# Two 1x1 convolutions of a residual block, both with seven products for eight, run in turn on halves of a tile

## The chip, the cores and the metric

The kernel runs on one core of a Trainium2 chip. The metric is the device time of one launch in microseconds (us); lower is better. Most runs of a kernel agree within 0.2%. Each result below is the median of four or five runs (three in the first table), one of them profiled.

## The reference, cut to what matters

Two residual blocks of the same shape follow each other, on an fp32 tensor of 64 images, 1024 channels, 14 x 14 pixels:

```python
def block(x, w1, b1, g1, be1, w2, b2, g2, be2, w3, b3, g3, be3, residual_scale):
    out = relu(bn(conv1x1(x, w1, b1), g1, be1))        # 1024 -> 256 channels
    out = relu(bn(conv3x3(out, w2, b2), g2, be2))      # 256 -> 256
    out = bn(conv1x1(out, w3, b3), g3, be3)            # 256 -> 1024
    return relu(x + softplus(residual_scale) * out)
# bn uses the mean and variance of the whole batch, so each convolution must end
# before its normalisation can start
```

## The kernel before: the parts the argument touches

A tile is two images (392 pixels, `PX`) of all channels, 32 tiles in all. The stages, in order: first convolution of block 0 ("first stage"); its 3x3 convolution; a Gram stage that gets the statistics of the third convolution without running it; then the **fused stage**, which runs the third convolution of block 0 and, on the tile just finished, the first convolution of block 1; then 3x3, Gram and third convolution of block 1.

The first convolution multiplies 2 x 2 blocks (channel halves by pixel blocks) with seven products for eight, in the manner of Strassen and Winograd. Its seven products share banks of PSUM: a running bank (`bu`, two of them in turn) into which P1, P6, P7 and P4 add one after the other, and a second shared bank (`bp`) for P5 and P3. Between two products on a bank ScalarE copies the partial sum out or VectorE evicts it. The pixel blocks are two whole tiles, so a matmul is 392 columns wide.

```python
# kernel before, fused stage (cut): third convolution plain, in tiles; first in pairs of tiles
def residual(psum, pool, b, t, w3, aff, made=()):
    ...
    for o in range(CS):                                   # 8 output groups
        ps = made[o] if o < len(made) else conv3(psum, t, o, w3)
        v = xt[:, o, :]
        nc.vector.scalar_tensor_tensor(v, ps, scale[:, o : o + 1], v, ALU.mult, ALU.add)
        nc.scalar.activation(v, v, AF.Relu, bias=shift[:, o : o + 1])
        ...
made = [conv3(psum, 0, o, w3) for o in range(2)]          # early, during the statistics
...
# kernel before, first stage (cut): order of the products, ScalarE not pinned
for t in range(2, T, 2):
    now.t23(); now.t1()                                   # sums of inputs on VectorE
    now.p2(); now.p6()
    ...
    after.p1()                                            # next pair
    now.p7(); now.p5(); now.c22(); now.p4(); now.p3()
```

`tc.keep_in_program_order` pins an instruction among the others so marked on its engine; without it a scheduler orders VectorE and ScalarE by its own forecast. Within one engine, instructions run in the order that results.

## Time and profile before

| of the kernel before | |
|---|---|
| time, median | 2220.75 us (2220.22 to 2221.67, 3 runs) |
| span of the profiled run | 2217.4 us |
| first stage, up to the first normalisation on ScalarE | 312.4 us |
| scaling of the Gram matrix to the next normalisation: statistics and fused stage | 760.0 to 1411.0, 651.0 us |

The prediction below shows the busy times, the windows and the instruction costs (its "fourth window" is the last of the three rows that it shows). Lines of the timeline: the columns are start, duration, engine, line, operation, output<-input, shapes, number of records, and in brackets the idle time before and what ended it. A record is one entry of the trace; each matmul in fp32 leaves two.

```profile
297.27 0.93 PE L126 MATMUL bu<-t,w1s 128*128 128x392 f32 x2 [0.64 <-ACT u L189]
...
767.83 3.63 PE L126 MATMUL bu<-zmean,w 128*128 128x2 f32 x32
771.32 2.16 PE L126 MATMUL bu<-ones,q 128*128 128x1 f32 x16
```

The first is from 30 to 309 us, where the first stage runs its seven products. The other two are the small matmuls of the statistics: 32 records in 3.63 us, 16 in 2.16.

### The profile page before, as it was taken

The numbers are of one execution on the slowest core, as the hardware profiler recorded it, in microseconds if no ns is written. First come the engines' busy times: TensorE is split into PE (matmuls) and PEld (weight loads), VectorE is DVE, ScalarE is ACT, GpSimd is POOL, SyncE is SP. The second block draws the span as 40 slices with busy tenths as digits, with TensorE's granted clock in tenths as the row PEclk, the third lists the DMA queues.
The fourth block names the chain that finished last, engine by engine and source line by source line (L and its number), as shares of the span: only waits on it lengthen the run. The fifth ranks groups of instructions, "written<-read, shape, count | busy, mean of one in ns | idle before, by whom it ended". The sixth has DMA issues, their size and how long they took to land.

```text
span 2217.4 us, 22513 instructions
## 1 busy us (share of the span) xinstructions
PE 2144.0 (97%) x8984; PEld 1578.6 (71%) x8984; DVE 1343.1 (61%) x2091; ACT 585.8 (26%) x943; POOL 60.9 (3%) x126
## 2 busy tenths in 40 slices
PE   8999979999989999999999999799999799999997
PEld 5555559999988855555555555599999797555554
DVE  4766567787775455554555555678878534444443
ACT  1111142111105032332223323511111221444443
POOL 0100000000001000000000000000000000000000
PEclk9999989999999999999999999899999899999999
DMA  7755425555543443443434432355555401778884
GB/s 276 267 204 206 176 84 190 187 193 190 187 158 121 159 167 149 171 175 145 175 152 171 171 146 116 148 186 194 190 186 194 195 12 59 291 290 302 306 319 176
DMA packets 43977, 409.13 MB, mean 185 GB/s; under 512 B 5216, under 2 KB 5472, under 8 KB 11104
## 3 DMA queue, kind: packets, MB, share of 16 engines
q1 hardware_dynamic: 29376, 286.80, 35.9%
q0 software_dynamic: 13056, 118.50, 13.1%
q10 hardware_dynamic: 1440, 2.40, 0.3%
q8 instruction: 71, 1.16, 0.2%
q14 instruction: 34, 0.28, 0.0%
HBM read 289.18 MB, written 118.49 MB: 184 GB/s over the span
## 4 chain that ended last, share of the span: by engine, by line
PE 83%; issue 12%; DVE 2%; ACT 1%; POOL 1%; DMA 1%; POOLq 0%; ACTq 0%; DVEq 0%; SPq 0%
PE ps L126 19%; PE bu L126 15%; PE bp L126 7%; PE ps L343 6%; PE ps L349 6%; PE ps L338 6%; PE ps L345 6%; PE ps L351 6%; PE bx L126 4%; PE bx L439 4%; PE bp L440 2%; PE ps L451 2%; ACT y L264 1%; POOL out L519 1%; DVE spare L155 0%
## 5 line engine op out<-in xcount | busy, mean ns | idle before, releaser
L126 PE MATMUL ps<-y,w 128*128 128x392 f32 x2048 | 685.6, 494 | 0.2 <-DVE x L515 0.2
L126 PEld LDWEIGHTS ps<-y,w 128*128 128x128 f32 x2048 | 390.4, 191 | 285.9 <-issue 2.8
L515 DVE SCALAR_TENSOR_TENSOR x<-ps,scale,x 128x392 f32<-128x392 f32 x512 | 316.0, 624 | 274.8 <-PE ps L126 273.5
L516 ACT ACTIVATE x<-x,shift 128x392 f32<-128x392 f32 x512 | 314.7, 622 | 435.5 <-DVE x L515 435.5
L371 DVE TENSOR_TENSOR f<-ps,ms 128x448 f32<-128x448 f32 x192 | 113.2, 600 | 148.3 <-PE ps L351 81.8
L338 PE MATMUL ps<-sums,u 128*128 128x224 f32 (+1 forms) x768 | 172.1, 347 | 25.4 <-DVE sums L318 12.7
L126 PE MATMUL bu<-t,w1s 128*128 128x392 f32 x496 | 173.6, 493 | 1.3 <-ACT u L189 1.3
L343 PE MATMUL ps<-r,u 128*128 128x224 f32 (+1 forms) x768 | 173.6, 347 | 0.0
L349 PE MATMUL ps<-r,u 128*128 128x224 f32 (+1 forms) x768 | 172.8, 346 | 0.0
L338 PEld LDWEIGHTS ps<-sums,u 128*128 128x128 f32 x768 | 137.3, 190 | 26.8 <-issue 13.3
L345 PE MATMUL ps<-r,u 128*128 128x192 f32 (+1 forms) x768 | 154.1, 322 | 0.0
L351 PE MATMUL ps<-r,u 128*128 128x192 f32 (+1 forms) x768 | 153.3, 321 | 0.0
L362 ACT ACTIVATE ms<-ps 128x448 f32<-128x448 f32 (+1 forms) x80 | 41.9, 524 | 391.7 <-PE ps L338 391.7
L126 PEld LDWEIGHTS bu<-t,w1s 128*128 128x128 f32 x496 | 94.1, 190 | 71.0 <-ACT u L189 2.8
L343 PEld LDWEIGHTS ps<-r,u 128*128 128x128 f32 x768 | 141.8, 190 | 1.3
L349 PEld LDWEIGHTS ps<-r,u 128*128 128x128 f32 x768 | 136.7, 189 | 1.4
L345 PEld LDWEIGHTS ps<-r,u 128*128 128x128 f32 x768 | 132.9, 189 | 1.2
L351 PEld LDWEIGHTS ps<-r,u 128*128 128x128 f32 x768 | 131.8, 188 | 1.0
L189 ACT ACTIVATE u<-bu 128x392 f32<-128x392 f32 x93 | 46.2, 497 | 303.2 <-PE bu L126 303.2
L439 PE MATMUL bx<-zt 128*128 128x257 f32 x392 | 119.3, 386 | 4.1 <-DVE zt L453 4.0
L453 DVE TENSOR_TENSOR zt<-ps,crow 128x512 f32<-128x512 f32 x98 | 66.2, 690 | 93.3 <-PE ps L451 93.2
L264 ACT ACTIVATE y<-y,shift,scale 128x1568 f32<-128x1568 f32 x64 | 103.6, 1682 | 6.4 <-DVE shift L556 6.4
(134 smaller groups left out, 2115.3 us busy)
## 6 DMA issues: line engine op xcount, KB each, us to landing
u<-u SPq DMA_DIRECT2D x96, 1280.0 KB, 5.5
x<-in_x SPq DMA_DIRECT2D x62, 1568.0 KB, 6.7
mid<-x POOLq DMA_DIRECT2D x32, 1568.0 KB, 5.5
x<-mid SPq DMA_DIRECT2D x32, 1568.0 KB, 8.5
out<-x POOLq DMA_DIRECT2D x32, 1568.0 KB, 7.7
u<-y POOLq DMA_DIRECT2D x24, 320.0 KB, 5.9
u<-spare POOLq DMA_DIRECT2D x24, 320.0 KB, 3.0
x<-in_x SPq DMA_DIRECT2D x4, 784.0 KB, 7.2
```

The costliest lines, as they stand in the source:

```text
L126: tc.keep_in_program_order(nc.tensor.matmul(*args, **kw))
L264: nc.scalar.activation(y, y, AF.Relu, bias=shift[:, s : s + 1], scale=scale[:, s : s + 1])
L338: nc.tensor.matmul(m[:, o, :n], w(s, D1D2), sums[:, s].rearrange("p l c -> p (l c)"), start=(s == 0), stop=(s == MS - 1),)
L343: nc.tensor.matmul(odd, w(s, D1), r[:, s, :, WH:], start=(s == 0), stop=False)
L345: nc.tensor.matmul(odd[:, :, : WH - 1], w(s, D3), r[:, s, :, WH + 1 :], start=False, stop=(s == MS - 1))
L349: nc.tensor.matmul(even, w(s, D2), r[:, s, :, :WH], start=(s == 0), stop=False)
L351: nc.tensor.matmul(even[:, :, 1:], w(s, D0), r[:, s, :, : WH - 1], start=False, stop=(s == MS - 1))
L371: nc.vector.tensor_tensor(f[:, o].rearrange("p r (i q c) -> p q (r i) c", i=GI, q=2)[:, :, :lines], eos[o][:, :, :n].rearrange("p q (l c) ...
L439: nc.tensor.matmul(g0, zt[:, c, 0:P], zt[:, c, :], start=first, stop=last)
L453: nc.vector.tensor_tensor(zt[:, :, :M], tp.rearrange("p (c m) -> p c m", c=CH), crow[:, None, :].to_broadcast([P, CH, M]), ALU.subtract,)
L515: nc.vector.scalar_tensor_tensor(v, ps, scale[:, o : o + 1], v, ALU.mult, ALU.add)
L516: nc.scalar.activation(v, v, AF.Relu, bias=shift[:, o : o + 1])
```

## The change

The intent: give the third convolution of the fused stage seven products for eight too. For that a tile is cut into two halves of 196 pixels, which serve as the pixel blocks; one matmul of the first convolution alternates with one of the third, the first lagging 42 products (28 of a tile and `LAG`) behind. A unit is one set of seven products of the third convolution, two of a tile's eight output groups; a tile has four. ScalarE's order is pinned, so that the relus of a unit stand behind the next unit's second copy; GpSimd takes two of the additions. One generator, `stream`, gives the order of products for both convolutions, so the first stage gets this order too, with whole tiles. Core of the diff, with cuts:

```diff
+LAG = 14
-    class Conv1:
+    class Seven:
+        def p1(self):
+            self.y = self.bank("y", 2)
+            yield from self.product(self.y, self.a[0][0], self.b[0][0], True)
+            self.after1()
 ...
+    def stream(items):
+        before = None
+        for now in items:
+            yield from now.p1()
+            if before is not None:
+                yield from before.p3()
+                yield from before.p4()
+            yield from now.p6()
+            if before is not None:
+                before.end()
+            yield from now.p2()
+            yield from now.p5()
+            yield from now.p7()
+            before = now
 ...
+    def act(*args, **kw):
+        tc.keep_in_program_order(nc.scalar.activation(*args, **kw))
 ...
+    class Conv1(Seven):
+        def after1(self):
+            self.u1 = self.saved("au1")
+            self.t1, self.t2, self.t3 = (self.sum(i) for i in range(1, 4))
+            nc.vector.tensor_sub(self.t3, self.b[1][1], self.b[0][1])
+            nc.vector.tensor_add(self.t2, self.t3, self.b[0][0])
+            nc.vector.tensor_sub(self.t1, self.b[0][1], self.b[0][0])
+        def after6(self):
+            self.u2 = self.saved("au2")
+            self.t4 = self.sum(4)
+            nc.vector.tensor_sub(self.t4, self.b[1][0], self.t2)
+        def after7(self):
+            self.result(1, 1, self.p, self.saved("au3"))
 ...
+    class Conv3(Seven):
+        def after7(self):
+            u3 = self.saved(...)
+            nc.gpsimd.tensor_add(self.part(1, 1), self.part(1, 1), u3)
+        def after3(self):
+            self.add(0, 1, self.p)
+            v = self.xt[:, self.o[0], :]
+            nc.gpsimd.tensor_add(v, v, self.u12)
+        def end(self):
+            for row in range(2):
+                self.relu(row)
 ...
+        a, c = stream(first_convs()), stream(last_convs())
+        step = 7 * CS // 2
+        for i in range(step + LAG):
+            next(c)
+        while True:
+            more = next(a, "end"), next(c, "end")
 ...
-                made = [conv3(psum, 0, o, w3) for o in range(2)]
+                    made = [conv3(psum, 0, o, w3) for o in range(2)] if b == 1 else ()
```

## The prediction

> **What bounds the kernel now.** I read the page's busy times first, then a table of windows cut at the stage borders, then the chain of waits, then single instructions on the timeline.
>
> ```profile
> PE 2144.0 (97%) x8984; PEld 1578.6 (71%) x8984; DVE 1343.1 (61%) x2091; ACT 585.8 (26%) x943; POOL 60.9 (3%) x126
> PE 83%; issue 12%; DVE 2%; ACT 1%; POOL 1%; DMA 1%; POOLq 0%; ACTq 0%; DVEq 0%; SPq 0%
> ```
>
> TensorE is busy for 97% of the span and carries the chain. The changed ("fused") stage, third convolution of layer 0 with first convolution of layer 1, is the fourth window; the first row is the first stage, which the change reorders. Columns: length, busy time with count per engine, granted clock, DMA share, GB/s.
>
> ```profile
> 0.00:310.00 310.00, 300.37 (x904) 172.70 (x904) 191.67 (x250) 45.78 (x87) 13.69 (x30) 1.00 0.56 204
> 760.00:781.00 21.00, 20.84 (x88) 13.46 (x88) 11.89 (x39) 1.77 (x5) 0.00 (x0) 0.92 0.22 77
> 781.00:1407.00 626.00, 624.33 (x1896) 359.58 (x1894) 331.96 (x429) 187.82 (x318) 17.01 (x32) 1.00 0.40 154
> ```
>
> In the fused window TensorE idles 1.7 of 626 us at full clock: the stage is its count of matmul records times their spacing. VectorE has half its time free, ScalarE 70%, and 154 GB/s leaves DMA out of it. Each fp32 matmul leaves two records. Spacing against width, from the chain (8 records) and from starts on the timeline (4 records a row):
>
> ```profile
> 43.84 2.63 PE bp L126 x8
> ...
> 650.45 0.73 PE L338 MATMUL ps<-sums,u 128*128 128x168 f32 x4
> 651.02 0.74 PE L343 MATMUL ps<-r,u 128*128 128x168 f32 x4
> ...
> 334.10 0.92 PE L338 MATMUL ps<-sums,u 128*128 128x224 f32 x4
> 334.85 0.93 PE L343 MATMUL ps<-r,u 128*128 128x224 f32 x4
> ```
>
> 392 columns: 2.634/8 = 329.2 ns a record. 168: 0.57/4 = 142.5. 224: 0.757/4 = 189.3. The new width, 196, lies midway: 166 ns, so 332 ns a matmul. Transposes of 128 columns follow each other at 0.44/4 = 110 ns, so weight loading does not limit 166. The engines that must follow have these costs (busy, mean ns):
>
> ```profile
> L515 DVE SCALAR_TENSOR_TENSOR x<-ps,scale,x 128x392 f32<-128x392 f32 x512 | 316.0, 624 | 274.8 <-PE ps L126 273.5
> L318 DVE TENSOR_TENSOR sums<-r 128x448 f32<-128x448 f32 x80 | 49.0, 617 | 0.6
> L219 DVE TENSOR_TENSOR t<-x 128x1568 f32<-128x1568 f32 x31 | 55.5, 1792 | 51.0 <-PE bu L126 38.6 <-ACT x L516 11.0 <-DMA x<-in_x 1.4
> L201 DVE BATCH_NORM_STATS2 stats<-y 128x6 f32<-128x392 f32 x124 | 70.3, 567 | 46.3 <-ACT y L196 43.7
> L189 ACT ACTIVATE u<-bu 128x392 f32<-128x392 f32 x93 | 46.2, 497 | 303.2 <-PE bu L126 303.2
> L196 ACT ACTIVATE y<-bu,par 128x392 f32<-128x392 f32 x31 | 18.2, 587 | 92.5 <-PE bu L126 92.5
> L516 ACT ACTIVATE x<-x,shift 128x392 f32<-128x392 f32 x512 | 314.7, 622 | 435.5 <-DVE x L515 435.5
> ```
>
> **What the Trainium skill says.** "ScalarE: Activation LUTs", section "What ACT_TABLE_LOAD costs": 186 ns + 0.833 ns per element, 93 ns more per per-partition operand, back-to-back instructions overlap by 93 ns. The trace agrees (497 without, 587 with). "VectorE: DVE Perf Modes", section "The TRN2 errata": an fp32 tensor_tensor takes (N+151)/0.96 ns; the trace has 617 against 624 at 448 and 1792 against 1791 at 1568. "GPSIMD Engine Reference", section 3.1: the same add takes 4497 ns at 2048 elements, 2.6 cycles an element. No GpSimd add is in this trace; scaled, my estimate is 0.5 us at 196 and 0.9 us at 392. "SBUF — State Buffer", section "Who interferes with whom": a VectorE instruction with two SBUF inputs and a GpSimd instruction that reads SBUF exclude each other. Nothing in the trace before can show this.
>
> **The change part by part.**
>
> Removed: the third convolution is now seven products for eight. Before, the fused work is 512 + 448 = 960 matmuls of 392 columns (four of them made early, during the statistics): 960 x 2 x 329.2 ns = 632 us. After, it is 896 + 896 = 1792 matmuls of 196 columns: 1792 x 332 ns = 595 us. **Minus 37 us.** The first convolution had seven products already; on halves of a tile it only pays the fixed part of twice as many records (448 x 658.4 = 295 against 896 x 332 = 297).
>
> Added per tile, where TensorE now needs 56 x 0.332 = 18.6 us. VectorE: 19 evictions of 196 columns (624 - 196/0.96 = 420 ns), three sums of 784 (970) plus a fourth, four of 196 (352), two statistics (567): 8.0 + 3.9 + 1.4 + 1.1 = 14.4 us, 77%. ScalarE: 13 copies with an operand (587 - 163 = 424), 3 plain ones (334), 8 relus (622): 5.5 + 1.0 + 5.0 = 11.5 us, 62%. GpSimd: 4 x (0.5 + 0.9) = 5.6 us. On average all fit under TensorE. What matters is the order, because these engines run theirs in turn and the banks that TensorE adds into are single (two only for the running product).
>
> So I walked one tile by hand through the built order (one matmul of each convolution every 0.663 us, reaction 0.2 us after an issue as in the trace, 0.07 us overlap on VectorE). The third convolution's copies return well before the next product on their bank. Two places are tight. (a) After the first convolution's seventh product VectorE runs two sums of 784, an eviction of the third convolution, then the eviction that frees the first's bank: 0.2 + 0.9 + 0.9 + 0.35 + 0.42 + 0.1 = 2.87 us, where TensorE returns after 2.98. It passes by 0.1. (b) After its fourth product: an eviction ends 0.29 after that border, then a sum of 784, a statistics instruction and an eviction, ready 2.1 us after, where the third convolution wants that bank after 1.99. About 0.14 us, 31 times: **plus 4 us**. If a GpSimd add of 0.5 us takes the shared port between the sums in (a), 0.4 us more: up to 12 us; I take half, **plus 6**.
>
> The start of the stage costs too. In the kernel before, TensorE fills the wait for the third normalisation with matmuls into spare banks:
>
> ```profile
> 773.34 6.95 PE L126 MATMUL ps<-y,w 128*128 128x392 f32 x16
> 773.51 0.18 DVE L500 COPY quad<-bu 128x24 f32<-128x24 f32 x1 [4.07 <-PE bu L126]
> 776.19 0.22 DVE L662 TENSOR_SCALAR scale<-scale,sp 128x8 f32<-128x8 f32 x1
> 780.46 5.83 PE L126 MATMUL ps<-y,w 128*128 128x392 f32 x17 [0.16 <-DVE x L515]
> ```
>
> After, the first product can run but the second adds into the same bank once ScalarE has copied it with the scale, known near 777 because small sums are mixed into the chain: about 4 us idle, and 0.8 us where the two early products stood: **plus 5**. Then 42 matmuls of the third convolution run alone; there third product, eviction (0.42), GpSimd (0.9), two relus (1.2) and a copy stand behind each other on ScalarE, some 0.7 us beyond the 2.3 us of a unit, six times: **plus 4**. Combining both weight sets late in the Gram stage puts eight additions of about 0.62 us on VectorE while TensorE needs its results every 1.75 us; transposes run ahead, so **plus 1.5**. At the end only the first convolution is left and (a) does not fit: **plus 1**.
>
> First stage: same matmuls at the same width in another order, and 300 of 310 us are TensorE. There (a) is one sum of 1.79 and an eviction against one product of 2.63 us, just enough. Its last pair loses two waits of 0.65 us on ScalarE's copies now, which the new order fills: **minus 1**. The row of constants loads separately, behind the normalisation chain: nothing. The mid store moves from GpSimd's queue to ScalarE's: one issue of some 0.5 us per tile, in slack.
>
> Sum: -37 + 4 + 6 + 5 + 4 + 1.5 + 1 - 1 = -16.5 to -17; 2220.75 - 17 gives **2204 us**, ratio 0.992.
>
> **The rivals.** First, everything hides: 4, 6 and 4 vanish, leaving -32 to 2189 us. For it: average loads of 77% and 62%; against it: margins of 0.1 us in walk (a) and (b), smaller than my error. Second, VectorE's order becomes the bound: if the port lock blocks sums repeatedly, or a GpSimd add takes 1.5 us, the relus move, then the next tile's sums and both tight places; at 1 us a tile the stage loses 31 us and the kernel stands at about 2225 us. For it: single banks and in-turn queues; against it: the order was pinned precisely so that the relus stand behind the next copies. Third, 196-column records cost more than 166 ns because of weight loading; 5% would be 30 us. Against it: 142.5 ns was reached at 168 columns.
>
> **Range and chances.** Eight in ten: 2188 to 2222 us. Faster by over 2% needs 2176 or less, 44 us, more than the whole removed TensorE work: 2%. Slower by over 2% needs 2265, some 2.6 us of stall a tile against my 0.3: 4%. Within 2%: 94%.
>
> **What would show it.** Fused matmul records of 196 columns starting 166 ns apart; a fused stage near 615 us; TensorE idle there behind VectorE releases of some 0.1 to 0.5 us once or twice a tile, above all before the products that add into the shared single bank; an idle of about 4 us before the stage; GpSimd adds of 0.5 and 0.9 us, VectorE's 784-sums longer than 0.97 when they meet them; the other stages unchanged to 2 us. I am wrong if the matmuls alone come out dearer, if ScalarE rather than VectorE is what TensorE waits for, or if the idle time in the fused stage is above 35 or below 5 us.

## The result, and the profile after

The changed kernel took **2213.38 us** (2212.45 to 2214.68, 4 runs) against 2220.48 us of the kernel before on the same chip (2219.4 to 2221.67, 4 runs). The ratio is 0.9968, 95% interval 0.9951 to 0.9986. The forecast gain was 16.5 us; the gain is 7. The page of the changed kernel, busy times and the chain of waits:

```profile
PE 2125.5 (96%) x10648; PEld 1808.1 (82%) x10648; DVE 1431.1 (65%) x2591; ACT 724.5 (33%) x1391; POOL 250.9 (11%) x350
...
PE 72%; issue 20%; DVE 4%; DMA 2%; POOL 1%; ACT 1%; POOLq 0%; SPq 0%; ACTq 0%
```

TensorE is still the engine that bounds the kernel, but the chain now spends 4% on VectorE where it spent 2%. The table of windows (length, busy time with count per engine in the order PE, PEld, DVE, ACT, POOL, then granted clock, DMA share, GB/s), for the first stage, the statistics, and the body of the fused stage:

```profile
0.00:312.00 312.00, 301.88 (x904) 170.77 (x904) 189.92 (x246) 43.81 (x85) 13.75 (x30) 1.00 0.55 201
...
762.00:784.00 22.00, 18.53 (x86) 14.53 (x86) 9.77 (x37) 0.89 (x3) 0.00 (x0) 0.78 0.15 48
784.00:1394.00 610.00, 603.20 (x3549) 587.68 (x3550) 416.75 (x918) 326.35 (x766) 206.82 (x256) 1.00 0.41 160
```

TensorE has 6.8 us of 610 free in the body where it had 1.7 of 626, and the clock of the statistics is 0.78 where it was 0.92. To see where the time went I took the same five marks in both traces (start of the first normalisation, start of the Gram stage's normalisation, start of the scaling of the Gram matrix, start of the normalisation after the fused stage, end):

| stretch | before, us | after, us | change | forecast |
|---|---|---|---|---|
| first stage | 312.44 | 316.53 | **+4.1** | -1 |
| 3x3 convolution, block 0 | 352.79 | 353.04 | +0.3 | 0 |
| Gram stage | 94.79 | 96.50 | +1.7 | +1.5 |
| statistics and fused stage | 650.98 | 639.26 | **-11.7** | -17 |
| the rest | 806.40 | 805.37 | -1.0 | 0 |
| sum | 2217.4 | 2210.7 | -6.7 | -16.5 |

So half of the missing 9.8 us was lost in the first stage, which the forecast had passed as "just enough", and half in the fused stage.

**The first stage.** TensorE now waits where the kernel before waited once. The timeline of the changed kernel at the first pair, at a filter piece and at the last pair:

```profile
32.67 1.26 PE L135 MATMUL ay<-at,w1s 128*128 128x392 f32 x3 [0.59 <-ACT au L234]
...
64.98 0.62 DVE L279 SCALAR_TENSOR_TENSOR y<-ap,par,au 128x392 f32<-128x392 f32 x1
...
65.65 0.93 PE L135 MATMUL ap<-x,w1s 128*128 128x392 f32 x2 [0.75 <-DVE y L279]
...
306.66 1.58 PE L135 MATMUL ap<-x,w1s 128*128 128x392 f32 x4 [1.31 <-DVE y L279]
```

`ap<-x,w1s` is P3, which adds into the shared bank after VectorE has evicted P5 from it (L279). I measured how much later than 0.329 us a record each product began: 0.86 at the first pair, 0.06 at almost every pair, 1.0 and 0.9 at 65.65 and 103.79, 0.3 at four more places behind filter pieces (parts of the 3x3 filter that VectorE and ScalarE transform beside this stage), 1.6 at the last pair: 6.2 us, against 0.9 before. TensorE started 1.2 us earlier; the difference is the +4.1. The first normalisation starts at 316.1 to 317.8 us in all ten profiles that have this first stage unaltered, and at 311.4 to 313.8 in the six that have the old one.

**The start of the fused stage.** Same view, around the statistics:

```profile
771.80 4.63 PE L135 MATMUL bu<-zmean,w 128*128 128x2 f32 x32
776.30 3.55 PE L135 MATMUL bu<-ones,q 128*128 128x1 f32 x16
...
784.08 1.02 PE L135 MATMUL cy<-ct,w3s 128*128 128x196 f32 x2 [2.93 <-ACT cu L234]
784.89 0.86 PE L135 MATMUL cx<-y,w 128*128 128x196 f32 x2
```

The same 32 and 16 records take 4.63 and 3.55 us where they took 3.63 and 2.16 (3.71 and 3.55 in the profile of the control run below), and the first products start 0.65 us apart, not 0.33: the granted clock is 0.50 from 774.2 to 787.9 us, and in the kernel before only from 772.8 to 776.3. The kernel before had twelve matmuls of the third convolution around there (four at 760 us, eight from 773 us), useful ones; the change took them away. The forecast has the 2.93 us wait (as "about 4") but no slow clock.

**The hand-over to both convolutions.** When the first convolution joins in, all four sums of its first tile stand together on VectorE, and two of them meet GpSimd:

```profile
802.04 1.67 DVE L288 TENSOR_TENSOR at<-at,x 128x784 f32<-128x784 f32 x1
...
803.74 1.25 DVE L306 TENSOR_TENSOR at<-x,at 128x784 f32<-128x784 f32 x1
...
805.38 0.60 PE L135 MATMUL cy<-y,w 128*128 128x196 f32 x2 [2.15 <-DVE x L341]
```

These sums take 0.97 us elsewhere. TensorE waits 2.15 us for an eviction behind them.

**The steady tile.** The stores of finished tiles are 18.90 us apart (median), against 56 x 0.332 = 18.58 us of matmuls. The 0.3 us lie in the two places that the prediction walked through. Here is (a), VectorE between the seventh product and P3:

```profile
1009.39 0.98 DVE L287 TENSOR_TENSOR at<-x 128x784 f32<-128x784 f32 x1
...
1010.40 0.98 DVE L288 TENSOR_TENSOR at<-at,x 128x784 f32<-128x784 f32 x1
...
1011.63 0.41 DVE L279 SCALAR_TENSOR_TENSOR y<-ap,par,au 128x196 f32<-128x196 f32 x1
...
1012.19 0.57 PE L135 MATMUL ap<-x,w1s 128*128 128x196 f32 x2
```

Two sums of 784 precede the eviction that frees the bank; P3 and the record after it come 0.11 and 0.08 us late. Place (b) costs 0.04 and 0.11 us. Over 31 tiles that is 10 us, the forecast 4 + 6.

### The profile page after: what moved, and what is told of

The parts are those of the page before. It is cut to its first block, busy times and chain, and to the rows that moved or that the text cites. A ratio compares the mean times of both kernels' runs of the same rounds, so it can differ in the third digit from the quotient of the medians.

```text
span 2210.7 us, 27233 instructions
## 1 busy us (share of the span) xinstructions
PE 2125.5 (96%) x10648; PEld 1808.1 (82%) x10648; DVE 1431.1 (65%) x2591; ACT 724.5 (33%) x1391; POOL 250.9 (11%) x350
## 4 chain that ended last, share of the span: by engine, by line
PE 72%; issue 20%; DVE 4%; DMA 2%; POOL 1%; ACT 1%; POOLq 0%; SPq 0%; ACTq 0%
PE ay L135 14%; PE cy L135 7%; PE ap L135 7%; PE ps L481 6%; PE ps L475 6%; PE ps L470 6%; PE ps L477 6%; PE ps L483 6%; PE cp L135 4%; PE ax L135 3%; PE cx L135 2%; PE bx L571 2%; PE ps L135 1%; DMA y<-in_w 1%; PE bp L572 1%
## 5 line engine op out<-in xcount | busy, mean ns | idle before, releaser
L135 PE MATMUL ps<-y,w 128*128 128x392 f32 x1024 | 339.1, 494 | 0.0
L135 PEld LDWEIGHTS ps<-y,w 128*128 128x128 f32 x1024 | 195.2, 191 | 142.8 <-issue 1.5
L645 DVE SCALAR_TENSOR_TENSOR x<-ps,scale,x 128x392 f32<-128x392 f32 x256 | 159.7, 625 | 174.2 <-PE ps L135 174.2
L234 ACT ACTIVATE cu<-cy,scale 128x196 f32<-128x196 f32 x384 | 158.7, 423 | 227.9 <-PE cy L135 225.4
L646 ACT ACTIVATE x<-x,shift 128x392 f32<-128x392 f32 x256 | 158.9, 622 | 177.4 <-DVE x L645 177.4
L135 PE MATMUL ay<-at,w1s 128*128 128x196 f32 (+1 forms) x752 | 209.7, 382 | 1.2 <-ACT au L234 1.0
L135 PEld LDWEIGHTS ay<-at,w1s 128*128 128x128 f32 x752 | 136.0, 190 | 36.6 <-ACT au L234 4.6
L234 ACT ACTIVATE x<-x,shift 128x392 f32<-128x392 f32 x256 | 145.5, 614 | 31.1 <-POOL x L367 29.3
L367 POOL TENSOR_TENSOR x<-x,cu 128x392 f32<-128x392 f32 x128 | 130.6, 1021 | 189.3 <-DVE x L341 187.0
L341 DVE SCALAR_TENSOR_TENSOR x<-cp,scale,x 128x196 f32<-128x196 f32 x256 | 106.8, 417 | 67.2 <-PE cp L135 67.2
```

What stands on the lines that cost most here:

```text
L135: tc.keep_in_program_order(nc.tensor.matmul(*args, **kw))
L234: tc.keep_in_program_order(nc.scalar.activation(*args, **kw))
L341: nc.vector.scalar_tensor_tensor(v, bank, self.scale[:, o : o + 1], v, ALU.mult, ALU.add)
L367: nc.gpsimd.tensor_add(v, v, self.u12)
```

## The experiments

Every run gives the right result unless it says otherwise. The edits are shown shortened. Each job has its own runs of the kernel before, and differences are given against the changed kernel, unaltered, which was run again as a control (its expectation first):

> The changed kernel once more, unaltered, as a control on the same chip and in the same rounds as the next three: about 2213.4 us, 0.9968 of the kernel before. It shows how far the medians of two jobs may differ.

Measured: 2213.25 us (2212.15 to 2213.56, 5 runs), ratio to the kernel before 0.9963 [0.9950, 0.9975]. Two jobs agree within 0.1 us in the median. Its profile, however, gives 623.5 us from the end of the scale and shift to the next normalisation, where the first profile of the same kernel gives 621.8: the clock fell once more, after the hand-over. So **profiles of one kernel differ by 1.7 us in this stretch**, and smaller differences of single profiles are not used.

### The old order in the first stage only

```diff
-            for _ in stream(items()): pass          # first stage, new order, ScalarE pinned
+            now = start(2); now.p1() ...            # class and loop of the kernel before
```

> The changed kernel with the old order of products, and the old unpinned ScalarE, in the first stage only; the fused stage stays new. If the new order is what costs the first stage its 4.1 us, the first normalisation starts near 312.4 us again (316.5 in the changed kernel) and the whole takes 4 us less than the changed kernel: about 2209.3 us. If that loss has another cause (the separate load of the constants, the filter pieces themselves), it stays within 1 us of 2213.4.

Measured: 2205.76 us (2205.38 to 2208.65, 5 runs), ratio 0.9930 [0.9918, 0.9942]. The first normalisation starts at 312.83 us. The loss of the first stage is the new order's, and of the forecast 4 us the trace shows 3.7. The medians differ by 7.6 us, more than the trace explains; the profiled run is the slowest of the five, so I take 4 as shown and the rest as open.

### ScalarE left free in the first stage

```diff
-            act(v, self.y, AF.Copy)
+            (act if self.n < PX else nc.scalar.activation)(v, self.y, AF.Copy)
```

The second `act` of the first convolution is changed in the same way.

> The changed kernel with ScalarE's instructions of the first stage left to the scheduler; the new order of products stays. If the pinned ScalarE (its copies held up behind the filter pieces) costs the first stage its 4.1 us, the first normalisation starts 2 us or more earlier than at 316.5 us, and the whole takes 2 to 3 us less. If the order of the products costs it (VectorE returns the shared bank too late), the start stays within 1 us of 316.5.

Measured: 2211.06 us (2210.35 to 2212.78), ratio 0.9955 [0.9941, 0.9968]; first normalisation at 315.6 us. The four late copies behind filter pieces are gone, 0.9 us; the waits at the first pair, the two for VectorE at 65 and 103 us and the last pair's stay. So the pinning is about a fifth of the loss, the order of products the rest. Of the 5.1 us of lateness that are left, about half is VectorE's (the two filter pieces and the 0.06 of most pairs); at the first and the last pair (2.4 us) a product directly follows the one whose copy it needs.

### VectorE pinned in the first stage, eviction ahead of the sums

```diff
-            nc.vector.tensor_add(self.t2, self.t3, self.b[0][0])      # after P1
+    def second(self):                                                # after the previous P3
+        tc.keep_in_program_order(nc.vector.tensor_add(self.t2, self.t3, self.b[0][0]))
+    # t1 after the previous P4; eviction and statistics pinned too; first stage only
```

> The changed kernel with VectorE held in program order in the first stage only, its sums spread over three products and the eviction of the shared bank ahead of them; the new order of products stays. Theory: apart from 0.8 us at the first pair, the first stage loses its 4.1 us to VectorE, which does sums before the eviction that frees the shared bank (0.06 us a pair, 1.3 at the last pair) or stands behind the filter pieces (0.8 twice); with the eviction first the first normalisation starts 2 to 3 us earlier, near 314 us. Rival: the filter pieces, whose data come late, stand in VectorE's order in any case; then the start stays within 1 us of 316.5, or it is later.

Measured: 2240.31 us (2237.07 to 2242.64, 4 runs), ratio 1.0087; the first normalisation starts at 343.9 us. My theory's remedy lost 27 us. At the pieces of the 3x3 filter, which VectorE and ScalarE transform beside this stage, TensorE waits up to 3.3 us, because the piece (which waits for its data and for ScalarE) now has a fixed place among VectorE's sums, and the second sum, one product later than before, keeps P6 waiting 0.5 us at other pairs. Four of the long waits are followed by a half clock, for 17 us in all, which costs another 8 of the 27. The rival was right that the pieces spoil a fixed order. The eviction placed first did take away the 0.06 us of most pairs, but the last pair still waits 1.3 us with no sum ahead of the eviction, so there the theory was wrong; that the order would have been enough without the pieces isn't shown.

### Filler around the statistics

```diff
-                    made = [conv3(psum, 0, o, w3) for o in range(2)] if b == 1 else ()
+                    made = [conv3(psum, 0, o, w3) for o in range(2)]     # unread for b == 0
                     conv3_stats(psum, pool, xpool, grams, w3, ccol, mv3)
+                    if b == 0:
+                        for o in range(2): conv3(psum, 0, o, w3)
```

> The changed kernel with four third convolutions of 392 columns put back as filler around the statistics (two before, two after; nobody reads them). Theory: the granted clock falls there because TensorE has too little work, so with filler the 32 records on zmean take 3.6 us again (4.6 now), the 16 on ones 2.2 (3.55 now), the first products of the fused stage start 0.33 us apart instead of 0.65, and the whole takes 3 to 4.5 us less than the changed kernel, about 2209.5 us. Rival: the low clock has another cause; the durations stay and the time is the same or up to 2 us longer.

Measured: 2214.02 us (2212.63 to 2214.2), ratio 0.9962 [0.9949, 0.9974]: no gain. The trace answers a part of the question of the clock:

```profile
775.21 3.63 PE L135 MATMUL bu<-zmean,w 128*128 128x2 f32 x32
778.70 2.11 PE L135 MATMUL bu<-ones,q 128*128 128x1 f32 x16
780.68 4.38 PE L135 MATMUL ps<-y,w 128*128 128x392 f32 x8
```

Both groups are back to their old times and the first products after them start 0.33 us apart. The clock is at half for 3.4 us here, as in the kernel before, and for 10.2 or 13.7 us in all thirteen profiles without any filler: wide matmuls behind the statistics bring it back. That those ahead of the statistics keep the 32 records fast is not shown. In nine of the sixteen profiles that lack them these records take 3.63 us too; the clock falls 2.3 to 3.8 us after the first of them there, and 5.1 here, but the filler also shifts them against the times at which the clock can change (see "Why the prediction was right or wrong"), and nothing separates the two. The time doesn't fall because the filler itself is on the path: 2.6 us ahead of the statistics, and behind them a second product that starts 1.2 us after the end of the filler. In the kernel before, the same matmuls were work that had to be done anyway.

### Filler only where TensorE waits for the scale

```diff
+        next(c)
+        spare = psum_tile(psum, PX, "ax").rearrange("p (h l) -> p h l", h=H)
+        for o, s in ((0, 0), (0, 1), (1, 0)):
+            matmul(spare, raw[:, s, o, :], two(0, s), start=True, stop=True)   # unread
-        for i in range(step + LAG):
+        for i in range(step + LAG - 1):
```

> The changed kernel with three matmuls of 392 columns that nobody reads behind the first product of the fused stage, where TensorE waits for the scale. Theory: they cost nothing there and bring the granted clock back, so the next twelve products start 0.33 us apart and not 0.65: about 2 us less in all, 2211 us; the statistics themselves keep their slow clock (4.6 and 3.5 us). Rival: the clock needs more work than this, and the time stays within 0.7 us.

Measured: 2211.52 us (2210.79 to 2212.44), ratio 0.9958 [0.9946, 0.9971]; the control has 0.9963, so no difference is shown. The first products do start 0.33 us apart (clock 0.95 from 784 to 788), but in this profile, as in the control's, the clock falls to half again for 3.4 us after the wait at the hand-over. With this filler the clock is at half for 10.2 us at the start here and for 6.8 in the two later runs that have it, against 10.2 or 13.7 without; its worth is within the noise.

### VectorE held in program order in the fused stage

```diff
-            nc.vector.tensor_sub(self.t3, self.b[1][1], self.b[0][1])
+            tc.keep_in_program_order(nc.vector.tensor_sub(self.t3, self.b[1][1], self.b[0][1]))
```

All evictions, sums and statistics of both convolutions in the fused stage are treated so, and the statistics of P4 move behind P6.

> The changed kernel with VectorE's instructions of the fused stage held in the order in which the program emits them, and the statistics of the first convolution one product later. So the eviction of the first convolution's shared bank comes before the three sums of 784, not after two of them. Theory: the two short stalls a tile are VectorE's order: the tile period falls from 18.90 us to 18.6 or 18.65 and the whole by 8 to 10 us, to about 2204 us. Rival: the stalls are the shared port of VectorE and GpSimd, or the reaction time between engines; then the period stays above 18.8 and the whole within 3 us of 2213.4.

Measured: 2226.36 us (2225.93 to 2228.14), ratio 1.0019 [1.0005, 1.0032], tile period 19.52 us: a miss by 20 us. The stall in (a) is gone and another takes its place:

```profile
1016.11 1.35 DVE L300 TENSOR_TENSOR at<-x 128x784 f32<-128x784 f32 x1
...
1018.38 0.97 DVE L302 TENSOR_TENSOR at<-x 128x784 f32<-128x784 f32 x1
...
1020.07 0.60 PE L135 MATMUL cp<-y,w3s 128*128 128x196 f32 x2 [0.69 <-DVE x L354]
```

Three sums now stand together (the middle one is left out), and the third convolution's evictions come behind all of them. The first sum takes 1.35 us because it meets GpSimd's addition.

### The same, with the sums spread over three products

```diff
             if before is not None:
                 yield from before.p3()
+                now.second()                      # t2 here
                 yield from before.p4()
+                now.third()                       # t1 here
```

> As the run with VectorE held in program order, but the three sums of 784 columns spread out, one after each of three products of the first convolution, so that no two stand together. Theory: the run before lost 0.86 us a tile because three sums in a row held up the third convolution's evictions, not because of the pinning; spread, no eviction waits more than one sum, the tile period falls from 18.90 us to 18.6 to 18.7 and the whole by 6 to 9 us, to about 2206 us. Rival: VectorE in a fixed order is too stiff whatever the order (each of its waits for ScalarE now stops it), and the period stays at or above 18.9.

Measured: 2206.08 us (2205.08 to 2206.78), ratio 0.9931 [0.9919, 0.9944], 7.2 us less than the control. The tile period is 18.78 us. In (a), the eviction now has no sum ahead of it:

```profile
1005.74 0.42 DVE L298 SCALAR_TENSOR_TENSOR y<-ap,par,au 128x196 f32<-128x196 f32 x1 [0.98 <-ACT au L245]
...
1007.33 1.34 DVE L311 TENSOR_TENSOR at<-x 128x784 f32<-128x784 f32 x1
...
1008.11 0.50 PE L135 MATMUL ap<-x,w1s 128*128 128x196 f32 x2
```

VectorE stands idle for 0.98 us before it, where the scheduler had put a sum, and TensorE is not late. Of 0.32 us of stalls a tile, 0.12 went, 3.7 us over 31 tiles. The end gave 0.5 (waits of 1.77 and 1.19 us in the changed kernel are 0.24, 0.92 and 1.19 here), the lone units about 1; the hand-over gave nothing, as a wait of 1.8 us for a sum took the place of that for an eviction. The rest lies in the start, where profiles of one kernel differ. So stall (a) is VectorE's order, as the theory said, and stall (b) stays (0.2 us a tile). My size for the steady part was twice the measured one; that the whole came out at 7 was partly luck.

### Without GpSimd's additions (a wrong result)

```diff
-            nc.gpsimd.tensor_add(self.part(1, 1), self.part(1, 1), u3)
-            nc.gpsimd.tensor_add(v, v, self.u12)
```

> The changed kernel without GpSimd's two additions a unit (a wrong result on purpose). Theory: they are off the path in the steady state, the period stays at 18.90 us within 0.05, and only the ramp of 42 products gets shorter by 1 to 3 us, so about 2211.5 us. Rival (the port shared by VectorE and GpSimd, half of the +6 in the prediction): the period falls by 0.15 us or more a tile, so 5 us or more in all, to 2208 us or less.

Measured: 2206.90 us (2206.52 to 2207.23), ratio 0.9932 [0.9919, 0.9944]. The period falls by 0.09 us to 18.81: between the two forecasts, 2.8 us in all. The hand-over loses 1.48 us instead of 2.42, and its four sums take 0.96 to 0.98 us each; the units before it lose about 1.1 us less, the end 0.5. So GpSimd costs 6 us in all, about half of it in the steady tile. The sums of the steady tile in the changed kernel are 0.96 to 0.98 us long and never run beside a GpSimd addition, so the shared port is not what costs there; by what way the 0.09 us a tile come is open.

### Relus two products later

```diff
             yield from now.p6()
-            if before is not None: before.end()
             yield from now.p2()
             yield from now.p5()
             yield from now.p7()
+            if before is not None: before.end()
```

> The changed kernel with the pinned relus of a unit two products later, behind the next unit's third copy, in the whole fused stage. Theory: in the 42 products that the third convolution runs alone, ScalarE stands at a relu that waits for GpSimd's addition of about 1.0 us, and the copy that TensorE waits for stands behind it (0.6 to 1.1 us a unit); later relus take 3 to 4 us off that ramp and nothing off the steady tile (18.90 us), so about 2209.8 us. Rival: the chain of eviction, GpSimd and copies is itself too long for a unit that runs alone, and the ramp stays within 1 us.

Measured: 2312.54 us (2311.64 to 2314.02), ratio 1.0416, a miss by 100 us. The ramp got worse as well, and the steady tile takes 21.4 and 23.0 us in turn. Rows of the timeline, then four of the table of windows, around one tile:

```profile
1000.93 1.68 DVE L287 TENSOR_TENSOR at<-x 128x784 f32<-128x784 f32 x1
...
1002.64 0.97 DVE L288 TENSOR_TENSOR at<-at,x 128x784 f32<-128x784 f32 x1
...
1004.10 0.92 PE L135 MATMUL ap<-x,w1s 128*128 128x196 f32 x2 [1.87 <-DVE y L279]
```

```profile
1003.00:1004.00 1.00, 0.00 (x0) 0.00 (x0) 1.00 (x3) 0.00 (x0) 0.00 (x0) 1.00 0.95 401
...
1006.00:1007.00 1.00, 1.00 (x5) 1.00 (x4) 0.13 (x1) 0.00 (x0) 0.00 (x0) 0.50 0.00 0
...
1004.20:1007.60 3.40, 3.40 (x11) 3.40 (x12) 0.50 (x2) 0.58 (x2) 0.08 (x1) 0.50 0.00 0
1007.60:1022.00 14.40, 14.40 (x88) 14.22 (x87) 8.59 (x21) 7.30 (x18) 4.81 (x7) 1.00 0.32 113
```

The sums read the finished tile, so later relus push them against the eviction and against GpSimd's addition (1.68 us). TensorE waits 1.9 us in every tile, and in **every second tile it then runs at half clock for 3.4 us**, 0.66 us a matmul; those are the tiles of 23.0 us. A wait of 1.9 us costs 3.6 there.

### ScalarE left free in the fused stage

```diff
-            act(v, v, AF.Relu, bias=self.shift[:, o : o + 1])
+            nc.scalar.activation(v, v, AF.Relu, bias=self.shift[:, o : o + 1])
```

All four `act` of the fused stage are treated so.

> The changed kernel with ScalarE's order in the fused stage left to the scheduler. If the pinned order is a gain, as it was meant to be, relus go ahead of copies that TensorE waits for, the tile period rises from 18.90 to 19.2 us or more, and the whole takes 10 us or more longer than the changed kernel. If the pinning costs something in the steady tile, the period falls to 18.7 and the whole by 5 us. Within 2 us of 2213.3: it doesn't matter.

Measured: 2254.26 us (2253.75 to 2254.8, 4 runs), ratio 1.0152, tile period 20.33 us. The scheduler starts two relus while the copy that TensorE wants next is still to come:

```profile
1006.16 1.18 ACT L346 ACTIVATE x<-x,shift 128x392 f32<-128x392 f32 x2 [2.85 <-POOL x L367]
...
1007.70 0.60 PE L135 MATMUL cy<-ct,w3s 128*128 128x196 f32 x2 [1.02 <-ACT cu L333]
```

So the pinning is worth 41 us in the fused stage: without it the change would be a loss of 1.5%.

### VectorE's additions in the six units that run alone

```diff
-            nc.gpsimd.tensor_add(v, v, self.u12)
+            self.engine.tensor_add(v, v, self.u12)      # nc.vector in the first six units
```

> The changed kernel with the two additions of the first six units of the third convolution on VectorE (0.36 and 0.56 us) in place of GpSimd (0.60 and 1.01 us); these are the units that run alone. Theory: ScalarE's relu waits for GpSimd there, and the copy that TensorE needs waits behind it; with the faster engine the 7.5 us of stalls fall by 3 to 4 us, as they fell by 2 to 3 without GpSimd, and the whole takes 3 us less than the changed kernel, about 2210.2 us; the steady tile stays at 18.90 us. Rival: the chain is long by its hops between engines, and less than 1 us comes back.

Measured: 2211.96 us (2209.27 to 2212.63), ratio 0.9959 [0.9945, 0.9972]; 621.5 us from scale and shift to the next normalisation. Nothing is gained that can be told from the noise. The waits in the lone units shrink (to 0.1 to 0.5 us in the third to fifth), but the sixth and the hand-over still wait 1.0 and 2.2 us, 0.2 less each than in the changed kernel: 1.2 us in all, where 3 to 4 were forecast. In this profile the slow clock at the start lasts to 790.7 us, not 787.9, and takes 1.0 us back. So the time is as the rival said, though more than 1 us came back in the units themselves.

### Versions put together

Old first stage and spread sums:

> The spread sums in the fused stage together with the old order of products in the first stage. If the two effects are independent, the gains add: 3.7 us of the first stage and 6 to 9 us of the fused one, to about 2202 us and some 0.5% faster than the changed kernel. If they aren't, less than 8 us in all.

Measured: 2200.94 us (2198.64 to 2201.54, 4 runs), ratio 0.9906 [0.9893, 0.9920]. The parts add: 12.3 us less than the control, where the spread sums alone gave 7.2 and the old order 3.7 (by the trace) to 7.5 (by the medians).

With later relus and filler added:

> Old order in the first stage, spread sums in the fused one, later relus and the three filler matmuls together. If their effects are separate they add: 3.7 + 7 + 3.5 + 2 us less than the changed kernel, about 2197 us, and 1.0% faster than the kernel before. If the later relus and the fixed VectorE order disturb each other in the steady tile, it stays at or above the 2201 us of the first two together.

Measured: 2218.40 us (2216.16 to 2220.2), ratio 0.9989; period 19.32 us. The later relus spoil it here too, by less: 0.54 us a tile over 18.78. The wait for VectorE's eviction is not there; what is new is a wait of 0.44 us for a copy of ScalarE, which is also in the run with later relus alone.

With VectorE's additions in the first units, and without and with the filler:

> As the run before, without the filler matmuls: about 2198 us. If the filler pays 1 to 2 us only where no stall of 2 us follows it (the run with filler alone got nothing in the end), this is 1 to 2 us longer than the run before; if filler never pays, it is the same or shorter.

> Old order in the first stage, spread sums in the fused one, VectorE's additions in the first six units, and the three filler matmuls. If all add up: 2201 us of the first two together, less 3 of the additions, less 1 to 2 of the filler: about 2196.5 us, 1.1% faster than the kernel before.

Measured: 2201.00 us (2198.7 to 2202.0, 4 runs), ratio 0.9910 [0.9897, 0.9924], without filler; 2198.99 us (2197.57 to 2200.95, 4 runs), ratio **0.9903** [0.9890, 0.9917], with it. Both forecasts were 2.5 to 3 us too low. In the first, the additions bring nothing; with the filler the median is 2 us lower, and the intervals overlap. Both beat the changed kernel and the kernel before; what they have in common with the run before, old first stage and spread sums, is what carries them.

## Why the prediction was right or wrong

The time fell inside the range, but the change was over-estimated by 9.8 us of 16.5. **The step that failed is the first stage**, which the prediction passed as "just enough" with a gain of 1 us at the last pair: it lost 4.1 us, half of the miss. The other half is a hand-over and a slow clock that no step had (5.6 us), and an end that was put too small, less what fell away elsewhere. By the prediction's steps:

- **Minus 37 for the products: right.** Records of 196 columns start 165.9 ns apart, so 1792 x 0.3318 = 594.6 us against 960 x 0.6584 = 632.1: 37.5 us.
- **Walks (a) and (b), plus 6 and plus 4: right in sum, by luck.** The stalls are 0.19 and 0.15 us a tile, 10 us in 31 tiles. The mechanism of the 6, half of a loss to the shared port, was wrong: no sum of the steady tile meets GpSimd. Walk (a) is simply too long by 0.1 to 0.2 us where I had it pass by 0.1: it takes 3.1 us in the trace, not 2.87, since the first sum starts 0.1 us later and the second, which reads the first one's result, starts only after its end. Spreading the sums took 3.7 us of the 10 away.
- **Start, plus 5: near in sum, partly by luck, with a part missed.** The wait for the scale is 4.2 us (0.6 and 3.6). Statistics are 3.4 us longer, 2.4 of it by the clock (1.5 in the control's profile), and the 3.7 us that the kernel before lost here and later in the stage (in part to a slow clock too, 773 to 776 us) fall away: 3.9 net. The slow clock then goes on through the first six products, 2.3 us that the prediction lacks.
- **Lone units, plus 4: right** (4.2), but the hand-over behind them loses 3.3 us, which no step foresaw. Nothing of it is a steady effect: it is four sums at once, two of them stretched to 1.67 and 1.25 us by GpSimd.
- **End, plus 1: too small**, 3.1 us.
- **Gram stage, plus 1.5: right** (1.7). The rest, 0: minus 1.0.
- **First stage, "just enough", minus 1: the step that failed.** It is +4.1 us, and putting the old order back returned 3.7. I walked the steady pair only. There it was indeed just enough, 0.06 us late; but the same walk with no slack loses 1.0 and 0.9 us where a filter piece stands in VectorE's queue. The first pair's P6 follows P1 directly and loses 0.86. The minus 1 was wrong twice: the kernel before has one wait of 0.64 us at its last pair (0.9 us late in all), not two of 0.65, and the new order does not fill it but loses 1.6 there, since P3 follows P7 directly.

These stage figures, 10 + 3.9 + 2.3 + 4.2 + 3.3 + 3.1 = 26.8 us of waits against 37.5 of products, give -10.7 for the fused stage where the marks give -11.7; the 1 us between is the error of adding up small gaps. Forecast were 20 us of waits.

Of the rivals, "everything hides" is out (its sum should read -30.5, not -32), and "VectorE's order becomes the bound" holds in kind, not in size: 0.3 us a tile, as the main line had it, not 1. The last rival, dearer records, is out.

The page "TensorE: Matmul & The Clock Gate" of the Trainium skill, section "Why this matters for your kernels", asks for no idle gaps of TensorE over about 3 us, and names the half rate that follows. I should have read it for the start of the stage. The runs agree on the half rate (clock 0.50, 0.65 us for 0.33), but here 1.9 us of waiting was enough in every second tile of the run with later relus, after the wait of 2.4 us at the hand-over it fell in two of the five profiles that have this stage unaltered, and it fell while TensorE counted as busy with 32 records of two columns. The page's section "What's actually happening" says that the clock is judged over free-running windows of 3413 ns. The traces agree: apart from the one at the end of a run, every stretch at half clock lasts 3.41, 6.83, 10.24 or 13.65 us, one to four such windows, and in a run they start whole windows apart. In the run with later relus fifteen of them start 44.37 us apart, 13 windows; two tiles of 21.37 and 23.05 us take as long, so the same wait falls alike every second time. Whether a wait of about 2 us costs a half clock thus depends on where it falls. "SBUF — State Buffer", section "Who interferes with whom", which the prediction had used, was right in the effect (sums of 1.25 to 1.68 us for 0.97 beside GpSimd), and told nothing of whether the two would meet.

## What to carry to other kernels

A margin that is just enough in the steady state is a loss at every irregular place: walk the first unit, the last one and every place where other work shares the queue before calling a step free, above all in stages the change touches only by sharing code. On a queue that runs in order, put the short eviction that frees a bank ahead of long sums and let no two long sums stand together; measure where a pinned order pays, since here pinning ScalarE was worth 41 us in one stage and pinning VectorE, with its sums spread, cost 27 in another. Waits of two microseconds on TensorE can cost as much again in clock, so ask which useful work filled a wait before an algorithm is swapped under it; here filler in its place won nothing that can be told from the noise.

## What the Trainium skill lacked or had wrong

- "TensorE: Matmul & The Clock Gate" gives some 3.4 us of idleness for the fall to half clock in its table of states, and no length for shorter idle times that do it too. Here a wait of 1.9 us was followed by 3.4 us at 0.50 in every second tile of one run, and the clock fell to 0.50 during matmuls of one and two columns that the profile counts as busy (4.63 us for 32 records, 3.63 where it fell behind them).
- "GPSIMD Engine Reference", section 3.1, has the addition at 2048 elements only; scaled, it gave me 0.5 us at 196 columns and 0.9 at 392. Measured alone: 0.60 and 1.01 us.
- "SBUF — State Buffer" says that VectorE and GpSimd exclude each other, without a size for additions. Here a sum of 784 columns took 1.35 us (0.97 alone) when GpSimd's addition of 392 columns had begun 0.50 us before it, 1.68 us when it had begun 0.16 us before, and that addition took 1.68 us (1.01 alone) when VectorE had begun.
- No page that I read has a size for how far profiles of the same kernel differ through falls of the clock in its middle: here 1.7 us in a stretch of 622 us.
